# A two-layer transformer on one core: the planned order takes in the load queue, and one number's sigmoid moves to the opening

## The chip, the cores and the metric

The kernel runs on one core of one Trainium2 chip. What counts is the device time of one execution, in microseconds (us); the time of a kernel is the median of its runs. A core has five engines that run their own instruction streams and wait for each other by semaphores: TensorE (PE, matmuls; its loads of the stationary operand are listed as PEld), VectorE (DVE), ScalarE (ACT), GpSimd (POOL) and SyncE (SP). SP does no arithmetic here: it issues the DMAs, that is the loads from and stores to the memory outside the core; POOL issues the indirect ones (gathers and scatter-adds of rows).

## The reference: what is computed

The input `x` has 8 sequences of 1024 rows of 256 numbers (f32). Two layers follow each other, each with four blocks, and each block adds its result to x after a layer norm:

```
x = x + attention_a0(ln(x))      # layer 0: attention in chunks of 64 rows, one head of 256
x = x + experts(ln(x))           # 8 experts, each takes 128 rows of every sequence
x = x + attention_b0(ln(x))      # Fourier chunks of 64: low part attention, high part convolution
x = x + experts(ln(x))           # the same experts again
x = x + attention_a1(ln(x))      # layer 1: linear attention of second order, 16 heads of 32
x = x + ffn(ln(x))               # three 256 x 256 products, bias, tanh
x = x + attention_b1(ln(x))      # window attention, 16 heads of 16, window 128
x = x + ffn(ln(x))
```

Of layer 0, what the change touches:

```
experts:  S = softmax(x Wg^T) over 8 experts; G, I = top 128 rows of each expert
          out[I] += G * (gelu(x[I] W1 + b1) W2 + b2)          # W1 256 x 1024, W2 1024 x 256
attention_b0, in chunks of 64 rows:
          X = rfft(chunk); low = X[:4], high = X[4:]
          A_low = block-causal attention(low) (16 heads of 64), real and imaginary parts alike
          H = pw(gelu(causal depthwise convolution of high, 7 taps dw)) * sigmoid(mean(chunk) gate_w^T)
          y = irfft(alpha * A_low + (1 - alpha) * low, H + high),   alpha = sigmoid(alpha_raw), one number
```

## The kernel before

All matmuls are in f32, and each is a step of some 128 x 128 blocks on PE. Layer 0 is written as a set of chains (Python generators), each of which asks for one piece of work after the other:

- `attention_a` (line 812 on) loads its weights `w1` and `bqk` (names in the trace: `w<-in_wqkv_a_dram`, `bqk<-in_bqk_a_dram`), then for 16 groups of four 128-row tiles it asks for a load of x (`x_a`, L829) and starts a `group`: layer norm on DVE and POOL (`ln4`, L439 statistics, L443 aggregate, L447 power on POOL, L452 apply), transposes on PE (`transposed`, L489; copies out L476 on ACT and L478 on DVE), q and k, v, scores, softmax, p v, and then a `tail`.
- `tail` normalises the result for the next block (tiles `txn_a`, `txn_b`), stores x and the normalised rows (L961, L970), transposes them and makes the routing logits (`put_logits`, L534 to L551).
- `route`, `expert_weights`, `expert_fetch` and `expert_work` are one round of the experts for a half of four sequences. The routing takes the softmax of the logits (`pr`, ACT exp at L581, DVE L582 to L584), transposes it on PE (L592), finds the top 128 on DVE and makes indices. The fetch gathers rows by POOL (L691, tile `xg`) and transposes them on PE (L489 again). The work is 8 `w1` steps (L722) with a gelu on ACT (L732), then `w2` steps (L761), gated on DVE (L771, tile `y`) and scattered by POOL (L778). Weights come through six buffers `we`, loaded by SP (L677). There are four rounds: two halves behind attention a, two behind attention b.
- `attention_b` (line 986 on) starts when all groups of attention a have been asked for and stored. It loads its weights by plain `load`s (helper at line 339, issue at L341) in this order: fourier, qw, kvw, ow, pw, gw, dw. Then it makes alpha:

```
alpha = w["alpha"] = wp.tile([P, 1], F32, tag="alpha", name="alpha")
nc.sync.dma_start(alpha, a["alpha"].partition_broadcast(P))                          # L1005
t = op("alpha", "ACT", 0.22, [], lambda: nc.scalar.activation(alpha, alpha, AF.Exp, scale=-1.0), table="exp")
def sigmoid():
    nc.vector.tensor_scalar(alpha, alpha, 1.0, None, ALU.add)                        # L1016
    nc.vector.reciprocal(alpha, alpha)
events["alpha"] = [op("alpha", "DVE", 0.15, [t], sigmoid)]
```

  The one reader is `dlow` (L1288), which scales the low part. Then, sequence by sequence, it starts chains of `spectrum`, the low attention (q, k, v, with the spread of k into `kbd` at L1228, scores L1309, softmax L1321, `low`), `convolution` (seven taps on DVE, L1369 and L1382), `gates` (sigmoid of the mean, L1418), `pw` and `hs` (L1133), and the inverse transform with its `tail`.

*What sets the order.* The class `Machine` (line 163 on) is a planner that runs while the program is built. It keeps a clock for each engine. Every piece of work has an engine, a cost in us (PE's in passes of 0.109 us), needs (earlier works), slots (numbered buffers) and a name; a load or a store has a `delay` until it has landed. `LAG` adds the time between an engine's end and another's start. In each turn `candidates` picks for each engine the work with the lowest start plus rank, where the rank is a number by name from `RANKS0` (layer 0) or `RANKS` (layer 1), adds 1.295 where ACT has to load another table, and 0.093 or 0.13 where a PE step has another tile shape than the one before. The earliest start of all is taken, and its instructions are issued. So the rank tables and the costs decide the whole order, on every engine.

The order in which the instructions are issued is kept for the engines named in one line (L1436): `with tc.manual_schedule(engines={EN.PE, EN.DVE, EN.Activation, EN.Pool}):`. SP is not among them: its loads and stores are placed by the framework's own scheduler. Loads that aren't asked of the planner (`load`) have no place in its clock; a step that reads such a tile waits for it by a semaphore, without the planner knowing.

Layer 1 (`layer1`, line 1441 on) has a planner of its own with the table `RANKS`, over loops of pairs of chunks. PE works there in three shapes: whole (128 x 128), rows (32 x 128 and the like) and columns (128 x 32). Its steps: transposes of normed rows (L1585), of k (L1806) and of `wt` (L1883), projections (L1765 to q and k, L1786 to v), `head_products` of q, k and u (L1663, the shape rows, four PSUM banks at once, which DVE empties with a mask each, L1671), sums over states and columns (L1689, L1701, L1717, L1727), the state (L1921, L1930), the output product `ho` (L2005), and the window attention's scores (L2144), transposes (L2215) and products (L2253).

Of the kernel before, what the change touches and what calls it, by code (L numbers as in the profile page):

```python
# [10 lines left out]
F32 = mybir.dt.float32  # L11
# [3 lines left out]
AF = mybir.ActivationFunctionType  # L15
ALU = mybir.AluOpType
# [4 lines left out]
P = 128  # L21
B = 8
S = 1024
D = 256
# [6 lines left out]
KS = 7  # L31
# [54 lines left out]
def _constants():  # L86
# [33 lines left out]
    "a add": 0.8, "a columns": -8.0, "a columns copy": -7.2, "a ex columns": 0.85, "a exp": -1.1,  # L120
    "a ln aggr": -2.75, "a ln apply": -0.65, "a ln pow": -0.6, "a ln stats": 0.4, "a max": 1.7,
    "a pt": -1.5, "a pv": -6.35, "a qk": 8.0, "a scores": 2.25, "a sum": -0.4, "a tail columns": -0.3,
    "a tail columns copy": 2.8, "a tail ln aggr": 0.25, "a tail ln apply": -1.55, "a tail ln pow": 3.5,
    "a tail ln stats": 2.0, "a v": 1.35, "a v bias": 1.9, "alpha": 1.1, "b add": -0.4, "b ex columns": 1.3,
    "b exp": -1.4, "b gelu": 0.1, "b k": -8.0, "b k spread": 6.1, "b ln aggr": -3.2, "b ln apply": 0.2,
    "b ln pow": -5.55, "b ln stats": 6.7, "b max": 5.05, "b ot": 6.55, "b pt": 4.45, "b pv": 5.2,
    "b q": -1.0, "b q scale": 2.0, "b scores": -0.4, "b spectrum": -6.25, "b spectrum copy": -2.8,
    "b sum": 2.9, "b tail columns": -4.55, "b tail columns copy": 2.0, "b tail ln aggr": -2.6,
    "b tail ln apply": 8.0, "b tail ln pow": -1.55, "b tail ln stats": 2.75, "b v": -2.15, "b v copy": -4.7,
    "b x add": -1.9, "convolution": 0.8, "cur": -0.85, "cv zero": 3.3, "dlow": -0.3, "gate": -1.6,  # L130
    "gates": -4.0, "gates add": -2.05, "gates exp": -4.1, "gates reciprocal": 6.45, "gates spread": 0.1,
    "gates store": 6.65, "hs": 6.95, "lo": 0.05, "load": -7.15, "logits": 6.15, "logits copy": 1.35,
    "low": 2.9, "lt": -6.6, "lt columns": 4.7, "mt": -7.65, "pr columns": -1.1, "pw": 5.05, "round": 1.95,
    "route exp": -1.15, "route max": 3.2, "route sum": -0.8, "scatter": -0.55, "store x": 1.6,
    "store xn": -0.1, "top": -0.05, "w1": 8.0, "w1 gelu": 5.95, "w2": 1.55, "weights": -0.7,
    "xg columns": 0.05, "xg columns copy": 1.3, "y": 6.1,
}
RANKS = {
    "bout": 4.6, "divide": 3.85, "dk": -0.25, "dq": -2.65, "dq scale": 0.8, "ex columns": 5.2, "exp": -0.4,
    "f_xt aggr": 7.15, "f_xt apply": -0.25, "f_xt columns": -1.35, "f_xt copy": 4.35, "f_xt pow": 2.75,  # L140
    "f_xt stats": -3.9, "ffn0": -4.05, "ffn0 add": 1.55, "ffn0 tanh": -1.4, "ffn1": 6.15, "ffn1 add": -1.6,
    "ffn1 tanh": 3.75, "fold": 8.0, "ho": 0.2, "ho add": 7.95, "in": -7.2, "kt": -3.75, "kt copy": 7.9,
    "kw": -7.6, "kw copy": 0.25, "l_xt aggr": -2.55, "l_xt apply": -0.65, "l_xt columns": 0.3,
    "l_xt copy": 0.8, "l_xt pow": 8.0, "l_xt stats": -3.55, "maximum": -6.3, "o0": 0.35, "ot copy": -0.45,
    "out": -0.3, "pt copy": -0.85, "pt second": 0.15, "pv": 3.9, "pv copy": -0.45, "qt": 5.55,
    "qt copy": 0.4, "reciprocal": 7.9, "scores": 0.15, "sk": -0.7, "sk mask": -0.2, "sp": -6.2,
# [183 lines left out]
def model(ctx: ExitStack, tc: tile.TileContext, a: dict, out: bass.AP):  # L330
# [29 lines left out]
    with tc.tile_pool(name="mk", bufs=1) as mk:  # L360
        mask_rows = load("mask_rows", [P, MASK_ROWS.shape[1]], a["masks"], pool=mk)
        for name, (lo, hi) in MASK_COLS.items():
            masks[name] = cpool.tile([P, hi - lo], BF16, tag=name, name=name)
            nc.vector.tensor_copy(masks[name], mask_rows[:, lo:hi])
# [2009 lines left out]
```

## Time and profile before

| | us |
|---|---|
| median of 3 runs (lowest, highest) | 3726.31 (3726.29, 3729.12) |
| the profiled execution, and its span | 3728.96, 3727.1 |
| PE busy in the span | 3580.6 (96%) |
| DVE, ACT, POOL busy | 2399.8 (64%), 1537.8 (41%), 1265.5 (34%) |
| PE busy from 0 to 30 us | 17.62 |
| PE busy from 30 to 315 (attention a) | 258.27 of 285 |
| PE busy from 315 to 430 (first routings) | 92.30 of 115 |
| PE busy from 430 to 630 (experts) | 200.00 of 200 |
| PE busy from 630 to 1300 (attention b and experts) | 641.03 of 670 |
| PE busy from 1300 to 1675 (last routings, experts) | 355.89 of 375 |
| PE busy from 1675 to 1800 (opening of layer 1) | 117.93 of 125 |
| PE busy from 1800 to 3640 (layer 1) | 1830.37 of 1840 |
| PE busy from 3640 to 3727 (its tail) | 67.15 of 87 |

The profile lists one execution. Its page has busy times, the span in slices and the chain of work that ended last; the trace behind it answers for windows of time, for waits (what an engine stood idle for, and what released it) and for the timeline (start, length, engine, line, what was written from what, and in brackets the idle time before and its releaser). The releaser is inferred from semaphores: where several ended a wait, the one that came last by the records is named. "PEclk" is the clock that TensorE was granted, 1.00 at full speed. An idle engine that isn't the bottleneck costs nothing.

### The profile page before, as it was taken

What the parts mean: (1) busy time and instruction counts of PE and PEld (TensorE: products, weight loads), DVE (VectorE), ACT (ScalarE), POOL (GpSimd) and SP (SyncE); (2) the same over time, 40 slices, a digit from 0 to 9 for tenths busy, and PEclk for the clock granted to TensorE, in tenths of its full rate; (3) what the DMA queues carried; (4) which work ended last, traced back from release to release, by engine and by line L of the source; (5) the groups of instructions that cost most, each with busy time, mean ns of one, the idle gap of its engine ahead of it and who ended that gap; (6) DMA issues with size and microseconds to landing.
All of it is one profiled execution on the core that took longest, in us unless ns stands there. A gap on an engine that the chain in (4) does not pass through costs nothing.

```text
span 3727.1 us, 101090 instructions
## 1 busy us (share of the span) xinstructions
PE 3580.6 (96%) x43080; PEld 2691.6 (72%) x43080; DVE 2399.8 (64%) x5653; ACT 1537.8 (41%) x4724; POOL 1265.5 (34%) x1326
## 2 busy tenths in 40 slices
PE   8898899999999999999999999999999999999997
PEld 5665566676677766667787878787778787878785
DVE  5576615675777672014777777777777777777776
ACT  2232223333143322212554555555555555555545
POOL 1003345242433245531233333333333333333334
PEclk9999999999999999999999999999999999999998
DMA  4213444334524344430000000000000000000000
GB/s 138 79 51 107 135 112 123 87 97 112 124 77 112 95 139 117 120 74 4 2 8 14 9 14 8 14 8 14 8 14 8 14 8 11 11 10 9 6 8 13
DMA packets 164145, 196.94 MB, mean 53 GB/s; under 512 B 11248, under 2 KB 141296, under 8 KB 163696
## 3 DMA queue, kind: packets, MB, share of 16 engines
q1 hardware_dynamic: 139120, 156.92, 13.5%
q0 software_dynamic: 24576, 33.57, 5.2%
q8 instruction: 339, 5.55, 0.6%
q14 instruction: 110, 0.90, 0.1%
HBM read 131.60 MB, written 58.85 MB: 51 GB/s over the span
## 4 chain that ended last, share of the span: by engine, by line
PE 48%; DVE 2%; ACT 1%; issue 0%; POOL 0%; POOLq 0%; DVEq 0%; ACTq 0%
PE acc L1765 5%; PE acc L1663 5%; PE acc L1701 5%; PE acc L2253 3%; PE acc L1616 3%; PE acc L2144 3%; PE acc L1786 3%; PE acc L2005 3%; PE acc L2215 2%; PE acc L1689 2%; PE acc L2274 2%; PE acc L1585 2%; PE acc L1727 2%; PE acc L2060 2%; PE acc L2035 1%; PE acc L1717 1%
## 5 line engine op out<-in xcount | busy, mean ns | idle before, releaser
L722 PE MATMUL acc<-xgt,we 128*128 128x512 f32 x1024 | 460.2, 602 | 0.0
L761 PE MATMUL acc<-we,ht 128*128 128x256 f32 x2048 | 454.6, 382 | 0.0
L2224 POOL TENSOR_TENSOR w_pt<-w_pt,w_above 128x512 f32<-128x512 f32 x256 | 322.7, 1275 | 338.8 <-ACT w_pt L2221 338.5
L2178 ACT ACTIVATE w_ex<-acc,w_nm 128x128 f32<-128x128 f32 x1024 | 362.1, 377 | 182.0 <-DVE w_nm L2170 114.8
L732 ACT ACTIVATE ht<-acc,b 128x512 f32<-128x512 f32 x256 | 175.8, 687 | 618.6 <-PE acc L722 618.1
L761 PEld LDWEIGHTS acc<-we,ht 128*128 128x128 f32 x2048 | 390.0, 192 | 53.8 <-issue 2.8
L722 PEld LDWEIGHTS acc<-xgt,we 128*128 128x128 f32 x1024 | 193.0, 193 | 223.3 <-issue 216.7
L1671 DVE TENSOR_TENSOR sk<-acc,consts 128x512 f32<-128x512 f32 x256 | 164.4, 682 | 157.2 <-PE acc L1663 157.2
L447 POOL TENSOR_TENSOR ln<-ln,nhalf 128x4 f32<-128x4 f32 x64 | 65.2, 1019 | 508.8 <-DVE ln L444 434.5
L1765 PE MATMUL acc<-l_xt,hw 128*128 128x256 f32 x1024 | 236.2, 384 | 0.8 <-ACT l_xt L1593 0.8
L2170 DVE TENSOR_REDUCE w_nm<-acc 128x2 f32<-128x256 f32 x512 | 217.5, 425 | 17.7
L2221 ACT COPY w_pt<-acc 128x512 f32<-128x512 f32 x256 | 141.0, 588 | 194.3 <-PE acc L2215 191.8
L2178 ACT ACTIVATION_READ_ACCUMULATOR w_ex<-acc,w_nm 128x1 f32 x1024 | 220.7, 216 | 0.0
L2195 DVE TENSOR_TENSOR w_ex<-w_ex,w_den 128x512 f32<-128x512 f32 x256 | 213.6, 834 | 8.8
L1765 PEld LDWEIGHTS acc<-l_xt,hw 128*128 128x128 f32 x1024 | 190.9, 191 | 31.4 <-ACT w_pt L2221 6.5
L771 DVE SCALAR_TENSOR_TENSOR y<-acc,gate,gb 128x256 f32<-128x256 f32 x128 | 60.7, 477 | 226.8 <-PE acc L761 178.7
L1671 DVE TENSOR_TENSOR sr<-acc,consts 128x512 f32<-128x512 f32 x256 | 161.2, 682 | 51.5 <-PE acc L1663 51.4
L778 POOL DMA_INDIRECT xa<-y,index x64 | 101.9, 1592 | 237.0 <-DVE y L771 229.3
L778 POOL DMA_INDIRECT xb<-y,index x64 | 101.7, 1589 | 229.9 <-DVE y L771 227.1
L1671 DVE TENSOR_TENSOR sp<-acc,consts 128x512 f32<-128x512 f32 x256 | 161.4, 683 | 14.8 <-PE acc L1663 14.7
L1956 POOL COPY state_bd<-state 32x128 f32<-32x128 f32 x224 | 64.1, 286 | 311.5 <-DVE state L1941 257.5
L1558 POOL TENSOR_TENSOR ln<-ln,nhalf 128x2 f32<-128x2 f32 x128 | 102.4, 800 | 198.7 <-DVE ln L1555 194.3
(260 smaller groups left out, 7902.6 us busy)
## 6 DMA issues: line engine op xcount, KB each, us to landing
we<-in_W_dram SPq DMA_DIRECT2D x128, 512.0 KB, 4.2
x_a<-in_x_dram SPq DMA_DIRECT2D x16, 512.0 KB, 4.4
xa<-x SPq DMA_DIRECT2D x16, 512.0 KB, 5.2
xna<-txn_a SPq DMA_DIRECT2D x16, 512.0 KB, 2.9
x_b<-xa SPq DMA_DIRECT2D x16, 512.0 KB, 4.8
gb<-g SPq DMA_DIRECT2D x32, 256.0 KB, 5.5
xb<-x_b SPq DMA_DIRECT2D x16, 512.0 KB, 2.8
xnb<-txn_b SPq DMA_DIRECT2D x16, 512.0 KB, 3.6
```

Source lines behind the costliest of these rows:

```text
L722: nc.tensor.matmul(ps, w1e[:, k, (f % 4) * P : (f % 4 + 1) * P], xgt[:, k, :], start=k == 0, stop=k == 1,)
L732: nc.scalar.activation(h, ps, AF.Gelu_apprx_tanh, bias=b1[:, col : col + 1])
L761: nc.tensor.matmul(ps[:, :D], ht[f][:, j * P : (j + 1) * P], r["w", e][2 + f // 4][:, f % 4, :], start=f == 0, stop=f == F // P - 1,)
L778: nc.gpsimd.indirect_dma_start(out=x_dram[HB * half + j][:], out_offset=bass.IndirectOffsetOnAxis(ap=index, axis=0), in_=rj["y"], in_offse ...
L1663: nc.tensor.matmul(ps[:, g * P : (g + 1) * P], lhs[rs, g, :], rhs[rs, g, :], start=True, stop=True)
L1671: nc.vector.tensor_tensor(dst, ps.rearrange("p (g t) -> p g t", t=P), bc4(const(mask)), ALU.mult)
L1701: nc.tensor.matmul(ps[32 * g : 32 * g + 32, 0:P], lhs(g, h), rhs[h][:, g, :], start=fresh, stop=i == len(cols) - 1, skip_group_check=True,)
L1765: nc.tensor.matmul(ps[:, gi * 256 : (gi + 1) * 256], hw[:, k, g * 384 + col : g * 384 + col + P], xt[:, k, :], start=k == 0, stop=k == 1,)
L2170: nc.vector.tensor_reduce(nm, sc[:, :, 0, :], AX.X, ALU.max, negate=True)
L2178: nc.scalar.activation(ex[:, 2 * jj + h, :], sc[:, h, 0, :], AF.Exp, bias=nm[:, h : h + 1], accum_out=den[:, 2 * jj + h : 2 * jj + h + 1],)
L2195: nc.vector.tensor_tensor(ex, ex, den.unsqueeze(2).to_broadcast([P, 4, P]), ALU.mult)
L2224: nc.gpsimd.tensor_tensor(pt[:, 1].rearrange("p (j h) t -> p j (h t)", j=2), pt[:, 0].rearrange("p (j h) t -> p j (h t)", j=2), above.rear ...
```

## The change

It has five parts.

1. SP joins the engines whose instructions keep the planner's order in layer 0.
2. Alpha is loaded and made at the very opening of the program, after the masks; `dlow` no longer names it as a need.
3. The weights of attention b become works of the planner on SP, each with a cost and a delay, in the order fourier, qw, kvw, gw, dw, ow, pw; the steps that read them name them as needs.
4. Costs: loads and stores of four tiles 2.6 to 3.0 us, "gate b2" 1.1 to 1.08 and a delay of 0.45, the state step "w" 12.2 to 12.4 passes, "o" 24.8 to 25.2, window "scores" 7.0 to 6.7 with the shape "rows" where "whole" stood; `LAG` gets an entry DVE to DVE of 0.12.
5. Both rank tables are replaced.

No arithmetic is added or taken away; the instructions are the same but for their order, and for table loads on ACT, of which the program holds 55 before and 41 after.

```diff
 RANKS0 = {
-    "a add": 0.8, "a columns": -8.0, "a columns copy": -7.2, "a ex columns": 0.85, "a exp": -1.1,
+    "a add": 0.75, "a columns": 1.6, "a columns copy": 0.9, "a exp": -3.5, "a ln aggr": -0.95,
...
 RANKS = {
-    "bout": 4.6, "divide": 3.85, "dk": -0.25, "dq": -2.65, "dq scale": 0.8, "ex columns": 5.2, "exp": -0.4,
+    "bout": 8.0, "divide": -0.05, "dk": 1.85, "dq": -7.8, "dq scale": 0.05, "ex columns": 2.85, "exp": -1.4,
...
     LAG = {
...
+        ("DVE", "DVE"): 0.12,
...
+    alpha = load("alpha", [P, 1], a["alpha"].partition_broadcast(P))
+    nc.scalar.activation(alpha, alpha, AF.Exp, scale=-1.0)
+    nc.vector.tensor_scalar(alpha, alpha, 1.0, None, ALU.add)
+    nc.vector.reciprocal(alpha, alpha)
...
-                                "weights", "SP", 2.6, [], lambda t=t, src=src: nc.sync.dma_start(t, src), delay=2.5
+                                "weights", "SP", 3.0, [], lambda t=t, src=src: nc.sync.dma_start(t, src), delay=2.5
...
-                        t_gb = op("gate b2", "POOL", 1.1, [("b2", s, half, e)], gated, ("gb2",))
+                        t_gb = op("gate b2", "POOL", 1.08, [("b2", s, half, e)], gated, ("gb2",), delay=0.45)
...
-                    alpha = w["alpha"] = wp.tile([P, 1], F32, tag="alpha", name="alpha")
-                    nc.sync.dma_start(alpha, a["alpha"].partition_broadcast(P))
...
-                    events["alpha"] = [op("alpha", "DVE", 0.15, [t], sigmoid)]
+                    w = {}
+
+                    def weight(name, shape, src, cost):
+                        t = w[name] = wp.tile(shape, F32, tag=name, name=name)
+                        events[name] = [op("weights b", "SP", cost, [], lambda: nc.sync.dma_start(t, src), delay=2.5)]
...
+                    weight("fourier", [P, FOURIER.shape[1]], a["fourier"], 3.6)
+                    weight("qw", [P, 2, 4 * D], rows_of("qw"), 5.2)
...
-                        t = yield step("b spectrum", 8, t_n, ("acc",) if h or k else ("acc", "xf"))
+                        t = yield step("b spectrum", 8, [*t_n, "fourier"], ("acc",) if h or k else ("acc", "xf"))
...
-                t = op("dlow", "DVE", 0.4, [t, "alpha"], scaled, ("dlow",))
+                t = op("dlow", "DVE", 0.4, [t], scaled, ("dlow",))
...
-            with tc.manual_schedule(engines={EN.PE, EN.DVE, EN.Activation, EN.Pool}):
+            with tc.manual_schedule(engines={EN.PE, EN.DVE, EN.Activation, EN.Pool, EN.SP}):
...
-                            "w0" if first else "w",
-                            8.4 if first else 12.2,
+                            8.4 if first else 12.4,
...
-                            t = yield step("scores", 7.0, needs, slots, feeds=2.2)
+                            t = yield step("scores", 6.7, needs, slots, "rows", 2.2)
```

## The prediction

> **What bounds the kernel now.** The page first: TensorE is busy 96% of a 3727.1 us span, and in the chain that ended last every other engine has 2% or less. So a time is lost or won here as TensorE's idle time, or as time between its matmuls. Second, the table of stretches, to see where the idle time lies (two of its rows here, layer 0's worst and the bulk of layer 1); its columns are the stretch, its length, the busy us of PE, PEld, DVE, ACT and POOL, then PE's granted clock, the DMA share and GB/s.
>
> ```profile
> 315.00:430.00 115.00, 92.30 (x461) 61.04 (x462) 62.20 (x162) 28.46 (x45) 46.77 (x44) 0.85 0.51 149
> ...
> 1800.00:3640.00 1840.00, 1830.37 (x32964) 1465.22 (x32959) 1362.67 (x3305) 970.58 (x3468) 626.56 (x702) 1.00 0.03 10
> ```
>
> Of 3727.1 − 3580.6 = 146.5 us idle, 12.4 lies before PE's first matmul (12.38), 9.6 the long stretch of layer 1 and 20 its last 87 us; nearly all the rest lies in layer 0, which ends near 1675. Third, what TensorE waited for in layer 0 (total us, times, longest):
>
> ```profile
> PE acc L592 <- DVE pr L584: 21.6, 3, 15.4
> PE acc L489 <- DVE txn_a L452: 17.3, 7, 2.8
> ...
> PE acc L489 <- DMA xg<-xnb,index: 12.4, 8, 4.1
> ```
>
> One wait of 15.4 us stands out. Fourth, the timeline around it (start, us, engine, line, what; idle before it in brackets):
>
> ```profile
> 386.24 1.31 SPq L1005 DMA_DIRECT2D alpha<-in_alpha_dram  x1
> ...
> 394.55 1.28 ACT L1011 ACT_TABLE_LOAD   x1 [17.15 <-DMA we<-in_W_dram]
> 395.84 0.20 ACT L1011 ACTIVATE alpha<-alpha 128x1 f32<-128x1 f32 x1
> 396.07 0.15 DVE L1016 TENSOR_SCALAR alpha<-alpha 128x1 f32<-128x1 f32 x1 [17.00 <-ACT alpha L1011]
> ...
> 401.21 1.87 PE L592 MATMUL acc<-consts,pr 128*32 128x128 f32 x8 [15.42 <-DVE pr L584]
> 402.87 5.69 PE L722 MATMUL acc<-xgt,we 128*128 128x512 f32 x8
> ```
>
> Read it from the bottom. PE waits for the probabilities `pr` of a routing; they stand on ACT and DVE behind alpha, a sigmoid of one number; alpha's load is the last of eight that SP issues from 378.72 (1 of 0.5 KB, 7.7 us from issue to landing). ACT stood still 17.15 us and DVE 17.00. The releaser named, `we`, isn't what ACT's line reads: L1011 reads alpha, and alpha's landing (386.24 + 7.7 = 393.9) fits its start. After the gap eight matmuls of L722 take 5.69 us, where eight before it took 3.60: a clock loss of 2.1.
>
> **The change part by part.** The sum stands against the profiled execution, 3728.96 us (span 3727.1 and 1.86 around it); it is 2.65 above the median 3726.31 and inside the three runs.
>
> *Alpha at the opening.* Gone from the middle: the 15.4 us wait and the 2.1 of half clock. What is late next: the routing's own chain. Counted from PE's arrival at 385.8 (401.2 − 15.4): a gelu in progress 0.69, a table load 1.28, exp 0.42, sum, reciprocal and product about 1.2, of which some 3.1 lies beside PE's work ahead of the step; 0.5 is left (0 to 4). So −17.0 (−13.5 to −17.5). At the opening alpha costs one DMA issue (about 0.45 on SP, as its neighbours there), 0.20 on ACT and 0.15 + 0.16 on DVE, in the wait for the first x: nothing. If that cover were gone, 0.5.
>
> *SP in the planned order.* Before, two loads of x stand ahead of the first layer's weights; in the built order of the new kernel both weights loads stand ahead of all x.
>
> ```profile
> 3.09 0.98 SPq L829 DMA_DIRECT2D x_a<-in_x_dram  x2
> ...
> 7.97 0.23 DVE L378 CAST ones<-on 128x128 bf16<-128x128 f32 x1
> 8.22 0.37 SPq L341 DMA_DIRECT2D w<-in_wqkv_a_dram  x1
> ...
> 8.82 1.41 DVE L439 BATCH_NORM_STATS2 ln<-x_a 128x6 f32<-128x256 f32 x4 [0.63 <-DMA x_a<-in_x_dram]
> ```
>
> The weights' load waits for the cast that ends at 8.20, so the first x goes out at about 9.1 instead of 3.1. It lands 4.4 later (median of x_a) at 13.5; its statistics began at 8.82. PE's start at 12.38 moves by that: +4.5 (2.8, if the mask lands sooner in a shorter queue; 6.5, if the 768 KB of weights ahead slow it). The weights of attention b go out at the same place, with at least 12 us of PE work between issue and first use; the first x of attention b has 5.3 us of PE work between issue and use (10 before) against 4.8 to land: 0 (0 to +2).
>
> *Layer 0 redrawn.* Every order on every engine comes from new rank tables, so each wait is looked up in the new order.
> - Attention a: seven waits of about 2.5 us (17.3) for `txn_a`, in a period of 20.5 us a group. DVE waits in its order for an x load (4.16 us in one group) with the tail's statistics behind it. In the new order these four statistics come first, so `txn_a` is ready about 2 us sooner, but in every second group its transposes also come sooner, right behind those of x. My chain by hand of two groups gives 40.2 us for 41.1: −0.5 a group, −4 over some eight (−10 to +2).
> - Gathers: the transposes of gathered rows (L489) wait for an indirect load. At the first (3.72), both experts' transposes stood ahead of the first w1; now four w1 steps stand between: −4 (−5 to 0). At two later ones, gaps of 4.07 and 3.84 now have two w1 (1.8 us) in them: −3.6 (−5 to 0).
> - The last routing: its gap near 1340 is 5.95, behind DVE copies for layer 1. PE's steps between the logits' transpose and the probabilities' grow from 3.6 us to some 7.5: −4 (−6 to 0).
> - Attention b: eight gaps, 18 us, partly for the spread of k (kbd), which stood behind 6-tap runs of 3.94 us on DVE. Now two convolution chains alternate and the spread stands ahead: −6 (−14 to +6, as these DVE chains also gate the pw step).
> - Tile shapes on PE: the new order changes shape 205 times where the old did 174, by 17 returns to the full shape. From rows of like steps, leaving the full shape costs 0.093 us (eight matmuls of 256 columns 1.729 to 1.822 until the next) and returning 0.056 to 0.104: +3.
>
> *Costs and lag.* Those constants are the planner's; no instruction has them. Their effect is the order, counted here.
>
> *Layer 1 redrawn.* It has nearly no idle time to win: 9.6 in 1840. Its shape changes go from 1140 to 1200, departures from the full shape from about 13 to 15 in each repeat of two chunks (63.3 us, about 30 repeats). The price of one full-shape step between others, start to start, in the old order:
>
> ```profile
> 2619.60 0.66 PE L1806 MATMUL acc<-consts,kt 128*128 128x128 f32 x4
> 2620.19 1.17 PE L1663 MATMUL acc<-qt,kt 32*128 32x128 f32 x32
> 2621.29 0.66 PE L1585 MATMUL acc<-consts,xn 128*128 128x128 f32 x4
> 2621.78 1.89 PE L2005 MATMUL acc<-ho,ot 128*128 128x256 f32 x8
> ```
>
> Four transposes take 0.59 to the next start when the shape changes (L1806) and 0.49 when it doesn't (L1585). Two more departures and returns a repeat: 2 × (0.12 to 0.21) = 0.24 to 0.42 us, +8.6 to +12.7 over 30 with the odd ones; up to 9 of idle time may close. I take +7 (0 to +14). The Trainium skill, "TensorEngine Tiling (Array Packing)", Key Properties, says that a change of tiling mode, not of the tile alone, drains the engine: a rule against this change. It gives no price; the row above agrees in sign at 0.1 us.
>
> Sum: −17 + 4.5 − 4 − 4 − 3.6 − 4 − 6 + 3 + 7 = −24.1; 3729.0 − 24.1 = 3704.9 on the profiled execution's scale. The median lies up to 2.65 lower, so I say 3704.
>
> The 2.1 us of half clock are seen once in these rows. The Trainium skill, "TensorE: Matmul & The Clock Gate", Part 1, says that an idle window of about 3.4 us halves the clock until about 3.4 us of work has passed, so about 1.7 us; by it, as an estimate, each of the four gaps of 3.7 to 5.95 above would give 1.7 more, and the sum would be some 7 lower.
>
> **The rivals.**
> 1. *The order closes most small waits.* If attention a gives its 10, attention b its 14, the gathers 10 and the last routing 6, with the +4.5, +3 and +7, it is −17 + 14.5 − 40 = −42.5: 3686. For it: each of these waits has a changed order ahead of it. Against: DVE's x_a loads stay just in time, about 4 us of PE work between issue and use, 4.4 to land.
> 2. *Only alpha counts.* The order wins nothing in layer 0 (a wait closed here opens there) and costs 4.5 + 3 + 7: −17 + 14.5 = −2.5: 3726. For it: some 89 us of idle time (146.5 less 12.4, 9.6, 20 and 15.4) stood in an order that keeps to the same dependences.
> 3. *The other side: PE waits for DVE in layer 1.* The new order moves the head products (L1663) close behind the projections of q and k; each takes four of eight PSUM banks, which DVE's masks (0.68 us each) free, and DVE is busy 74% there (1362.67 of 1840). A wait of w a repeat adds 30w; the sum passes +7.5 at w = (24 + 7.5) / 30 = 1.05 us. At 1.35, two masks' time, it is −24 + 40 = +16: 3745. Against: DVE has 16 us of slack in a repeat, and before only 9.6 us of idle show in the whole stretch.
> 4. *The change doesn't do what it says.* Alpha goes, but `pr` is as late, since the redrawn ACT queue has other work ahead of it, or it waits behind the eight loads in another form. Then alpha gives 0 to −4: −24 + 15 = −9, 3720. Against: nothing in the built order ahead of that exp names alpha or those weights.
>
> **How the numbers follow.** Forecast (3690 to 3718) 0.50; rival 1 0.12; rival 4 0.10; rival 2 0.15; rival 3 0.13. Three runs of one kernel spread by 2.8 us, so I hold 0.2%, 7.5 us, for what can be told from no change: faster is below 3718.9, slower above 3733.8. Faster: 0.50 + 0.12 + half of rival 4 and a fifth of rival 2, 0.70; same: the rest of these two, 0.17; slower: 0.13. Eight in ten of the chance lie from 3680 (rival 1 with one more of its bounds) to 3732 (rival 2 with layer 1's +14), which leaves rival 3 out. The likeliest case by itself is 3690 to 3718.
>
> **What would show it.** In the new profile: no alpha line after 15 us; the wait of L592 on `pr` near 390 under 4 us, and eight L722 after it at 3.6 us; PE's first matmul near 16.9; fewer than seven `txn_a` waits of over 2 us; the two 4 us gather gaps near 2; the routing gap near 1340 under 3; PE busy in the long stretch of layer 1 above 99.4%, its length grown by about 7. It is wrong if that stretch grows by tens of us (rival 3), or if a wait of over 10 us stands again near 390 (rival 4).

## The result, and the profile after

The changed kernel takes 3674.02 us (median of 4 runs, 3671.57 to 3675.74) where the kernel before takes 3726.79: a ratio of 0.9855, with a 95% interval from 0.9842 to 0.9867. That is 52.8 us less, and faster by 6 us than the lower end of the predicted range. In two later sessions the same changed kernel took 3680.46 and 3680.48 beside 3728.17 and 3727.99 for the kernel before, so a difference of under some 7 us between sessions says nothing; variants are compared below with a run of the same session where there is one.

The profiled execution took 3672.32 us. The first part of its page, the span and TensorE's busy time:

```profile
span 3670.5 us, 101245 instructions
...
PE 3570.6 (97%) x43080; PEld 2678.6 (73%) x43080; DVE 2379.5 (65%) x5653; ACT 1521.4 (41%) x4710; POOL 1332.2 (36%) x1326
```

Two things moved that the diff does not name: PE is busy 10 us less with the same matmuls, and POOL 67 us more with the same instructions. The table of stretches after the change (stretch, length, busy us of PE, PEld, DVE, ACT, POOL, then PE's granted clock, DMA share, GB/s). Layer 1 starts at 1623.1 now (1675.4 before), so its bulk is 1748 to 3588:

```profile
0.00:30.00 30.00, 12.72 (x37) 6.98 (x38) 14.58 (x60) 5.41 (x8) 4.22 (x10) 1.00 0.80 264
300.00:430.00 130.00, 119.67 (x528) 81.69 (x527) 90.92 (x183) 32.31 (x53) 61.80 (x56) 0.95 0.54 154
...
1748.00:3588.00 1840.00, 1835.24 (x32818) 1467.34 (x32810) 1357.10 (x3307) 973.12 (x3470) 626.17 (x702) 1.00 0.03 10
3588.00:3670.00 82.00, 57.41 (x612) 40.37 (x608) 53.20 (x136) 43.16 (x170) 39.75 (x33) 0.89 0.03 11
```

The first routings have lost half of their idle time and their slow clock (0.95 for 0.85); the bulk of layer 1 has 4.8 us idle for 9.6. What PE waited for in layer 0 (total us, times, longest; a line number is 4 higher than before, 9 lower from attention b's middle on):

```profile
PE acc L493 <- DVE xn_a L456: 17.3, 1, 17.3
PE acc L493 <- DMA xg<-xnb,index: 10.0, 7, 2.2
PE acc L1057 <- DVE xn_b L456: 7.4, 5, 2.2
PE acc L493 <- DMA xg<-xna,index: 6.2, 4, 3.9
...
PE acc L493 <- DVE txn_a L456: 5.7, 11, 1.1
PE acc L596 <- DVE pr L588: 3.2, 1, 3.2
```

Of the same list before the change, three lines that are compared with it:

```profile
PE acc L489 <- DMA xg<-xna,index: 8.3, 7, 3.7
PE acc L1152 <- DVE hs L1133: 7.9, 4, 3.6
PE acc L1309 <- DVE kbd L1228: 7.1, 4, 1.8
```

No wait on `pr` of 15 us, none on `kbd` or `hs`; the opening is longer. The longest wait for a gather of the first half, `xna`, is as long as before (3.9 for 3.7). The timeline of the routing that stood behind alpha:

```profile
369.02 5.32 PE L726 MATMUL acc<-xgt,we 128*128 128x512 f32 x12
...
371.11 0.42 ACT L585 ACTIVATE pr<-pr 128x256 f32<-128x256 f32 x1
...
372.40 0.42 DVE L588 TENSOR_TENSOR pr<-pr,sm 128x256 f32<-128x256 f32 x1
...
374.17 1.04 PE L596 MATMUL acc<-consts,pr 128*32 128x128 f32 x8
...
375.04 5.32 PE L726 MATMUL acc<-xgt,we 128*128 128x512 f32 x12
```

The probabilities are there 1.3 us before PE asks for them, and twelve matmuls behind take 5.32 us where eight took 5.69. And the opening:

```profile
6.63 0.23 DVE L382 CAST ones<-on 128x128 bf16<-128x128 f32 x1
...
6.89 0.38 SPq L341 DMA_DIRECT2D w<-in_wqkv_a_dram  x1
...
7.82 4.69 SPq L833 DMA_DIRECT2D x_a<-in_x_dram  x5
...
13.72 1.41 DVE L443 BATCH_NORM_STATS2 ln<-x_a 128x6 f32<-128x256 f32 x4 [6.59 <-DMA x_a<-in_x_dram]
...
17.28 2.30 PE L493 MATMUL acc<-consts,xn_a 128*128 128x128 f32 x8 [17.28 <-DVE xn_a L456]
```

The first x goes out behind the weights, at 7.82 (3.09 before), and PE starts at 17.28 (12.38).

Put against the prediction's own terms, from the two traces (idle time of PE in front of each kind of matmul, and for the rest the time from each matmul's start to the next start, idle time taken off):

| term | predicted, us | measured, us |
|---|---|---|
| wait for alpha's routing | −14.9 | −15.4 |
| opening | +4.5 | +4.9 |
| attention a: waits on txn_a, ex_a, logits and the like (23.96 to 15.30) | −4 | −8.7 |
| gathers of `xna`, the first among them (8.34 to 6.18) | −4 | −2.2 |
| gathers of `xnb`, the two later gaps among them (12.36 to 10.03) | −3.6 | −2.3 |
| last routing and the two others beside alpha's (6.21 to 3.23) | −4 | −3.0 |
| attention b: hs, kbd, xn_b, ex_b, pt_b (21.85 to 7.87) | −6 | −14.0 |
| small waits (indices, logits) | 0 | −2.1 |
| layer 0, start to start: clock behind alpha −2.1, shapes +3 | +0.9 | −9.6 |
| layer 1: idle −3.5, start to start −0.8 | +7 | −4.3 |
| sum | −24.1 | −56.7 (span: −56.6) |

In the three profiles of the changed kernel the rows of idle time repeat within 1 us, apart from the late copies named at the end of this text; the start-to-start figures do not. Layer 0's start-to-start time is 1565.1 us here and 1560.4 in another profile with the same old layer 0 (the run with layer 1 alone), and 1555.5, 1557.6 and 1559.3 in the three profiles of the changed kernel. So its −9.6 may be anything from −1 to −10. Layer 1 as a whole takes 2051.7 us before, and 2047.5, 2051.6 and 2048.4 in the three profiles of the changed kernel: −4.3 is the largest difference that these give.

### The profile page after: what moved, and what is told of

Its sections match the earlier page's. It is cut to its first block, busy times and chain, and to the rows that moved or that the text cites. A ratio compares the mean times of both kernels' runs of the same rounds, so it can differ in the third digit from the quotient of the medians.

```text
span 3670.5 us, 101245 instructions
## 1 busy us (share of the span) xinstructions
PE 3570.6 (97%) x43080; PEld 2678.6 (73%) x43080; DVE 2379.5 (65%) x5653; ACT 1521.4 (41%) x4710; POOL 1332.2 (36%) x1326
## 4 chain that ended last, share of the span: by engine, by line
PE 88%; DVE 6%; DMA 2%; issue 2%; POOL 1%; ACT 0%; SPq 0%; POOLq 0%; DVEq 0%; ACTq 0%
PE acc L765 11%; PE acc L726 11%; PE acc L1756 6%; PE acc L1654 6%; PE acc L1692 5%; PE acc L2206 3%; PE acc L1777 3%; PE acc L2244 3%; PE acc L1996 3%; PE acc L2135 3%; PE acc L1607 3%; PE acc L1680 2%; PE acc L2265 2%; PE acc L851 2%; PE acc L1718 2%
## 5 line engine op out<-in xcount | busy, mean ns | idle before, releaser
L2215 POOL TENSOR_TENSOR w_pt<-w_pt,w_above 128x512 f32<-128x512 f32 x256 | 332.9, 1316 | 362.3 <-ACT w_pt L2212 362.3
L1756 PE MATMUL acc<-l_xt,hw 128*128 128x256 f32 x1024 | 245.4, 389 | 1.5 <-ACT l_xt L1584 1.5
L2169 ACT ACTIVATION_READ_ACCUMULATOR w_ex<-acc,w_nm 128x1 f32 x1024 | 228.8, 223 | 0.0
L1549 POOL TENSOR_TENSOR ln<-ln,nhalf 128x2 f32<-128x2 f32 x128 | 89.9, 702 | 367.9 <-DVE ln L1546 293.3
L2158 DVE COPY_PREDICATED acc<-consts,acc 128x128 f32<-128x128 int32 x512 | 147.0, 287 | 22.9 <-PE acc L2135 22.5
```

The costliest lines, as they stand in the source:

```text
L1756: nc.tensor.matmul(ps[:, gi * 256 : (gi + 1) * 256], hw[:, k, g * 384 + col : g * 384 + col + P], xt[:, k, :], start=k == 0, stop=k == 1,)
L2169: nc.scalar.activation(ex[:, 2 * jj + h, :], sc[:, h, 0, :], AF.Exp, bias=nm[:, h : h + 1], accum_out=den[:, 2 * jj + h : 2 * jj + h + 1],)
L2215: nc.gpsimd.tensor_tensor(pt[:, 1].rearrange("p (j h) t -> p j (h t)", j=2), pt[:, 0].rearrange("p (j h) t -> p j (h t)", j=2), above.rear ...
```

## Experiments: alpha

**Alpha alone.** The kernel before, with this part of the change and no other:

```diff
+    alpha = load("alpha", [P, 1], a["alpha"].partition_broadcast(P))
+    nc.scalar.activation(alpha, alpha, AF.Exp, scale=-1.0)
+    nc.vector.tensor_scalar(alpha, alpha, 1.0, None, ALU.add)
+    nc.vector.reciprocal(alpha, alpha)
...
-                    alpha = w["alpha"] = wp.tile([P, 1], F32, tag="alpha", name="alpha")
-                    nc.sync.dma_start(alpha, a["alpha"].partition_broadcast(P))
```

> The kernel before with alpha loaded and made at the opening; rank tables, costs, SP and weights as before. Theory 1 (the 15.4 us wait of L592 and the half clock behind it, 2.1 to 2.6, are alpha's alone and nothing takes their place): 16 to 18 us less than before, 3709 to 3711; PE's first matmul stays near 12.4. Rival (the probabilities would be late anyway, on ACT or DVE or behind the loads of attention b's weights): a wait of over 5 us stays there and the gain is under 12 us, 3715 or more.

Measured: 3709.46 beside 3726.23, a ratio of 0.9958 (0.9944 to 0.9972), 16.8 us. In the timeline of this run PE's idle time there is 0.89 (15.42 before):

```profile
385.03 0.42 DVE L588 TENSOR_TENSOR pr<-pr,sm 128x256 f32<-128x256 f32 x1
385.60 1.03 PE L596 MATMUL acc<-consts,pr 128*32 128x128 f32 x8 [0.89 <-DVE pr L588]
386.47 5.32 PE L726 MATMUL acc<-xgt,we 128*128 128x512 f32 x12
```

The prediction's 0.5 us of remaining wait and its −17 hold (the interval is 10 to 21 us). Layer 0's idle time falls by 13.6 us here (110.3 to 96.7). Its start-to-start time reads 1560.9, but the run with layer 1 alone, of the same session and with the 15.4 us gap still in it, has 1560.4; so the 2.1 us of slow running behind the gap are all that is shown of it.

**Alpha put back.** The changed kernel with alpha's load and operations at the start of attention b again; PE's order is the same, instruction for instruction.

> The changed kernel with alpha's load and its three operations put back to the start of attention b, PE's order the same instruction for instruction. Theory 1: the wait for the second routing's probabilities is back at 8 to 16 us with up to 2.6 of slow clock behind it, the time is 10 to 18 us above the changed kernel's 3674. Rival (the new order hides alpha's load): within 4 us of 3674.

Measured: 3683.07. The wait for `pr` is back with 3.74 us, less than 8 to 16, since alpha's load now goes out ahead of attention b's weights, which are the planner's works by then, and not behind seven of them. Against the changed kernel's 3674.02 this is 9 us, against its later sessions 2.6: an estimate of alpha's worth inside the new order lies between these. The changed kernel was not run beside this variant, so the wait of 3.74 us is the better figure. Most of the 15.4 us lay in the place at the end of the load queue.

## Experiments: the opening and SP's order

**x first.** The changed kernel, with the first two loads of x sent ahead of attention a's weights:

```diff
-                    w1 = load(
-                        "w1", [P, 2, 3 * D], a["wqkv_a"].rearrange("(k p) e -> p k e", p=P), pool=wpool
-                    )
-                    bqk = load("bqk", [P, 4], a["bqk_a"], pool=wpool)
+                    def fetch(x, g):
+                        nc.sync.dma_start(x, x_rows[g])
+                        if g == 1:
+                            nc.sync.dma_start(w1, a["wqkv_a"].rearrange("(k p) e -> p k e", p=P))
+                            nc.sync.dma_start(bqk, a["bqk_a"])
```

> The changed kernel with the first two loads of x ahead of the loads of attention a's weights, as they stood before; PE, ACT and POOL in the same order. Theory 1 (the opening's 4.9 us are the order of these loads): PE's first matmul back at 12.4 from 17.3, the time 4.9 us less, 3669. Rival (the weights then come late and the loss moves to the first projection): PE's first matmul near 12.4, a wait of 3 to 5 us at the first projection, and the time within 2 us of 3674.

Measured: PE's first matmul at 12.28, no wait at the first projection, the experts' first step at 321.2 (326.4): the opening is as predicted. But the time was 3678.29, 4.3 more than the 3674.02, and there was no run of the changed kernel in that session. So it was run again:

> The changed kernel itself, beside the others on the same chip, as the yardstick for differences of a few us from it. If the 4 us that the run with x first lost are that kernel's, this one stays within 2 us of 3674; if they lie in the chip or the hour, it is at 3677 to 3679.

Measured: 3680.46. The same kernel thus differs by 6.4 us between two sessions, and the 4.3 us of the variant are within that. What x first is worth in time by itself, no run of one session shows.

**More loads behind x.** As x first, with the loads of `rows`, the gate's weight and the first bias behind it too.

> The changed kernel with the first two loads of x ahead of attention a's weights and of the loads of rows, gate and first bias too; PE, ACT and POOL in the same order. Theory 1: x goes out 1.3 us sooner than in the run with x first, PE's first matmul at 10.9 to 11.5 instead of 17.3 to 18.2, the first step of the experts 6 us sooner than 327, and the time 5 to 7 us less than the changed kernel beside it. Rival (mask and weights bind then): PE starts sooner but waits for the weights, at most 4 us gained.

Measured: first matmul at 11.04, the experts' first step at 321.0, the time 3674.62 in a session without the changed kernel; against 3680.5 of the sessions around it, 5.9 less, which is within what sessions differ by.

**SP free again.** The changed kernel with SP left out of the engines that keep the planner's order; 48 lines of SP's order differ, and none of PE, ACT and POOL. Its yardstick, the changed kernel in the same session, comes first:

> The changed kernel itself, the yardstick for the three others on this chip: 3672 to 3681, where its runs have been so far.

> The changed kernel with SP left out of the engines that keep the planner's order, as before; PE, ACT and POOL in the same order, 48 lines of SP's differ. Theory 5 (SP's part of the change costs the opening and gives nothing): PE's first matmul back near 12.4, no load of x, of weights or of attention b late, the time 0 to 5 us less than the yardstick. Rival (the planned order of loads and stores is what lets the new order run): waits for x or weights come back, 5 us or more above the yardstick.

Measured: 3673.44 beside 3680.48, 7.0 us less. The first rows of PE in the two timelines, this variant and then the yardstick:

```profile
12.75 1.66 PE L493 MATMUL acc<-consts,xn_a 128*128 128x128 f32 x5 [12.75 <-DVE xn_a L456]
```

```profile
17.51 1.87 PE L493 MATMUL acc<-consts,xn_a 128*128 128x128 f32 x6 [17.51 <-DVE xn_a L456]
```

So the part of the change that the title names first costs the opening, 4.8 us, and no run shows it to give anything back. The runs of the two kernels overlap a little (3672.1 to 3677.9, and 3676.5 to 3684.1), so I count 5 to 7 us. The whole change is faster in spite of it.

## Experiments: attention b

The trace after the change shows something that the prediction had named but not priced. Before, the seven taps of one convolution chain follow each other on DVE, each waiting for the last. After, two chains alternate. The groups of taps, before and after (count, busy us, mean ns, idle):

```profile
L1382 DVE SCALAR_TENSOR_TENSOR cv<-xf,dw,cv 128x448 f32<-128x448 f32 (+2 forms) x192 | 126.6, 660 | 6.6
```

```profile
L1373 DVE SCALAR_TENSOR_TENSOR cv<-xf,dw,cv 128x448 f32<-128x448 f32 (+2 forms) x192 | 106.8, 628 | 0.0
```

From start to start, first taps included and idle time taken off, that is 0.627 us each before and 0.544 after, 18.6 us over 224; with the idle time, some 0.04 us between two taps of one chain, it is 0.656 before. What lets the planner see it is the entry of 0.12 us from DVE to DVE in its table of lags: two works in line on one engine no longer look as if they could follow at once, so the next tap of another chain is picked first. That is read from the code; no run takes the entry out. Two runs take the taps by themselves. The places of the taps in DVE's order are kept, and only which tap is issued in which place is changed:

```diff
-                        t = op("convolution", "DVE", 0.365, [*needs, "dw"], first)
+                        taps.append(first)
+                        t = op("convolution", "DVE", 0.365, [*needs, "dw"], issue)   # issue: taps.pop(0)()
```

**Serial taps in the changed kernel.**

> The changed kernel with the convolution's taps on DVE put back one chain after the other in the same places of DVE's order; every other instruction of every engine stands where it stood. Theory 2 (what empties attention b's waits is that two chains of taps alternate, 0.544 us a tap for 0.627 in the traces): DVE busy grows by 15 to 19 us, waits at the scores or the inverse transform return, and the time is 6 to 14 us longer, 3680 to 3688. Rival (the place of the spread and of hs in DVE's order does it, the taps lie beside PE's work): at most 3 us longer.

Measured: 3703.44 beside 3680.46, 23 us longer, more than the 6 to 14 expected. What PE waits for from 560 us to layer 0's end in this run, and then in the yardstick:

```profile
PE acc L1143 <- DVE hs L1124: 15.4, 6, 2.7
PE acc L493 <- DMA xg<-xnb,index: 10.5, 8, 2.2
PE acc L1057 <- DVE xn_b L456: 9.4, 5, 3.0
```

```profile
PE acc L493 <- DMA xg<-xnb,index: 9.9, 7, 2.2
PE acc L1057 <- DVE xn_b L456: 7.8, 5, 2.8
```

The wait for `hs` is there with 15.4 us. Layer 0's idle time grows by 18.3 us (69.0 to 87.3) and its start-to-start time by 10.7.

**Alternating taps in the kernel before.**

> The kernel before with the same taps alternating between two chains in the same places of DVE's order, nothing else moved. Theory 2: DVE busy falls by 15 to 19 us, the waits of kbd (7.1 us in all) and hs (7.9) go for the most part, 8 to 14 us less than before, 3713 to 3719. Rival: waits stay, within 3 us of 3727.

Measured: 3724.05 beside 3728.17, a ratio of 0.9991 (0.9982 to 1.0), so a gain of 0 to 7 us where 8 to 14 were expected. The waits of `kbd` are gone and those of `hs` fall from 7.9 to 1.6, as theory 2 has it. But two new ones of 6.9 us come. The timeline at the first:

```profile
617.25 1.89 POOL L691 DMA_INDIRECT xg<-xna,index  x1 [0.30 <-issue]
...
619.45 9.76 POOL L691 DMA_INDIRECT xg<-xna,index  x1 [0.30 <-issue]
621.03 0.81 DVE L1374 TENSOR_SCALAR cv<-xf,dw 128x464 f32<-128x464 f32 x2
621.76 6.62 DVE L1388 SCALAR_TENSOR_TENSOR cv<-xf,dw,cv 128x448 f32<-128x448 f32 x12
...
631.29 0.21 POOL L1099 COPY lo<-xf 128x48 f32<-128x48 f32 x1
...
631.56 2.72 PE L1199 MATMUL acc<-lo,qw 128*128 128x128 f32 x11 [6.88 <-POOL lo L1099]
```

A gather on POOL takes 9.76 us, as long as DVE runs taps without a pause; in the kernel before, the same gather beside serial taps takes 0.95:

```profile
617.83 0.95 POOL L691 DMA_INDIRECT xg<-xna,index  x1 [0.30 <-issue]
```

Behind it on POOL stand the copies of the low part `lo`, and PE waits for these. In the changed kernel the same happens eight times (5.65 us twice, 9.56 six times; the sum over all gathers and scatters is 396 us for 333, which is 63 of POOL's 67 us of added busy time), but there PE's list has no wait for POOL, so nothing that PE needs soon stands behind the gather. So neither the taps nor the order alone gives attention b's 14 us of idle time: the new order needs quick taps (23 us without), and quick taps in the old order gain 4.

## Experiments: attention a

**A sixth buffer for x.** The kernel before, with one number changed (22 lines of PE's order follow):

```diff
-                    "x_a": 5, "xn_a": 2,
+                    "x_a": 6, "xn_a": 2,
```

> The kernel before with six buffers for x in attention a instead of five, so that each load goes out a group earlier; 22 lines of PE's order differ. Theory 3 (DVE waits in its order for a load of x that is just in time, the tail's statistics wait behind it, and txn_a is late for that): the seven txn_a waits (17.3 us) fall below 4 in all, and with what runs slowly behind each (1.1 us of eight transposes at 1.73 for 1.04 and the like) 14 to 22 us less than before, 3705 to 3713. Rival (DVE has too much to do between, the load only covers it): the waits keep more than half, under 8 us gained, 3719 or more.

Measured: 3723.61 beside 3728.17, a ratio of 0.9986 (0.9978 to 0.9995). The waits on `txn_a` keep 15.4 of 17.3 us. The edit did not do what it was for: the planner starts a group's statistics as early as its load allows, so with a buffer more DVE waits for the load of a later group in the same place (3.94 us, for 4.16). The theory is not tested by it. The experts' first step comes at 319.0, 8 us sooner, of which about 4 are idle time.

**The tail's statistics first.** The kernel before with two ranks of the new table:

```diff
-    "a ln stats": 0.4, "a tail ln stats": 2.0,
+    "a ln stats": 1.3, "a tail ln stats": 0.9,
```

> The kernel before with two ranks of the changed kernel's table, so that DVE takes the tail's four statistics ahead of those of x in attention a; 148 of 13438 lines of PE's order move with it, all in attention a. Theory 3 (the tail's statistics queue behind DVE's wait for a load of x, and txn_a is late for that): the txn_a waits (17.3 us in seven) fall below 6 in all, attention a ends 8 to 16 us sooner, 3711 to 3719. Rival (the late txn_a only hands its wait to the next step in line, as the buffer and tap runs did): the sum of idle time in attention a falls by less than 5 us, 3722 or more.

Measured: 3734.24 beside 3729.73, a ratio of 1.0012 (1.0004 to 1.0021): slower. What PE waits for in the first 600 us:

```profile
PE acc L534 <- DVE txnt_a L478: 15.6, 5, 7.2
PE acc L634 <- DVE idxf L630: 13.7, 1, 13.7
...
PE acc L489 <- DVE txn_a L452: 7.4, 11, 1.1
```

The theory holds where it was meant: `txn_a` is ready sooner (7.4 us for 17.3), and between its first matmul and 300 us PE stands idle 8.1 us for 22.3 before. The 14 us are lost again after it. The five waits for `txnt_a` (15.6) all lie between 316 and 338 us, where the first routing's search for the top 128 (L614 to L624 on DVE) now stands between the copies of the last tails. The 13.7 us in front of the indices are alpha's wait in another place: DVE stands still 12.75 us at L1016 for alpha, up to 353.0, and the indices' cast follows at 353.27; the wait of 15.4 us for `pr` is not in this list. No run joins these two ranks with alpha at the opening.

**Attention a's ranks put back in the changed kernel** (the names that begin with a; 172 of 13438 lines of PE's order differ):

> The changed kernel with the ranks of attention a alone (the names that begin with a) put back; 172 of 13438 lines of PE's order differ, all in attention a. Theory 6 (the new order of attention a is itself worth what its idle time fell by, 8.6 us, and the slow running behind): the first step of the experts comes 8 to 14 us later than the yardstick's 327, the time is 8 to 14 us longer. Rival (the lag and the corrected costs, which stay, did it): within 3 us.

Measured: 3695.48 beside 3680.48, 15.0 us longer; layer 0's idle time is 14.2 us more. The mark that was set, a later first step of the experts, failed (316.4, sooner, as the order of the two works changes too); the end of the first round of experts comes 16.5 us later. So attention a's order as a whole, with the first routing that runs into it, is worth some 15 us inside the changed kernel. Which of its ranks bring this, no run takes apart.

**A sixth buffer in the changed kernel,** and then together with x first:

> The changed kernel with six buffers for x in attention a instead of five. Before the change this gave 8 us up to the first step of the experts (319.0 for 327.1). Theory 3b (DVE's wait for x is still in the new order): the first step of the experts comes 4 to 8 us sooner than 327. Rival (the new order has taken that gain): within 2 us of 327, the time as the changed kernel's.

Measured: first step at 321.1, 6 us sooner than 327; the time is 3679.47, nothing to tell from the yardsticks of other sessions.

> The changed kernel with both edits that brought the experts' first step forward by 6 us each: x loaded first, and six buffers for x. Theory 7: they add, the first step is at 315 to 316, and 4 to 8 us remain at the end, 3668 to 3674 where the yardstick is at 3676 to 3680. Rival (what is won early is lost again by the end of layer 0, as each alone lost most of it): within 3 us of the yardstick.

Measured: first step at 316.8 (9.5 us sooner than the yardstick's 326.2), 3674.07 beside 3680.48, 6.4 us less. It is no faster than SP free alone: what is won early is lost in part by the end of layer 0.

## Experiments: layer 1

**Layer 1 alone.** The kernel before with the new `RANKS`, three costs and the lag there; its layer 0 is the old one in every instruction's place.

> The kernel before with the changed kernel's layer 1 alone (its rank table, its three costs, the lag between two operations of DVE there); layer 0 as before. Theory 1, from the two traces (layer 1 takes 2051.7 us before and 2047.4 after): 4.3 us less than before, 3722. Rival, the prediction's own price (each more return to the full shape paid in full): 7 us more, 3734. A second rival, that layer 1 gains only behind the new layer 0: no difference, 3727.

Measured: 3722.07 beside 3726.23, a ratio of 0.9989 (0.9980 to 0.9998), so 4.2 us less (0.7 to 7.5): near the traces' 4.3, and the other sign than the prediction's +7. Layer 1's idle time shows it in every profile: 29.0 to 30.7 us in the five with the old order, 23.9 to 26.2 in the twelve with the new one. Its start-to-start time does not tell the two apart (2020.2 to 2023.5 us, and 2021.3 to 2025.7). The prediction's count of shape changes was the mistake. Taken from all changes of shape in the two traces of layer 1 (mean of the time from the last matmul of a group to the next start, over the usual distance in that group; F is 128 x 128, R 32 x 128, C 128 x 32):

```
change       before            after             sum after - before
F to R      223 x  94 ns      254 x  93 ns       +2.7 us
F to C      113 x  95 ns      140 x  93 ns       +2.4
R to F      255 x 220 ns      280 x 216 ns       +4.4
C to F      161 x 199 ns      195 x 188 ns       +4.8
C to R       96 x 193 ns       65 x 192 ns       -6.1
R to C       33 x 205 ns        7 x 237 ns       -5.1
F to F      589 x  44 ns      560 x  33 ns       -7.2
```

The prediction counted 59 departures and 59 returns, priced a little low at 8.6 to 12.7 us together (14.3 here). It left out that 57 of them stand where a direct change stood, and that such a change costs as much as a return: −11.2. What stays of the shapes is +3 (2.5 to 3.6 between any two profiles of the two orders). Steps that change no shape give −7.2, most of it at the ffn's bias matmuls, for a reason that no run here isolates; but layer 1's start-to-start time as a whole falls by only 0.8 in these two profiles, and in most other pairs it does not fall. The Trainium skill, "TensorEngine Tiling (Array Packing)", Key Properties, says that a change of mode drains the engine. The runs are in line with it, and put the numbers beside it: some 0.09 us to leave the full shape, some 0.2 to return, and some 0.2 between two others.

**Fewer changes of shape.** The changed kernel, with the planner's price of a change tripled in layer 1:

> The changed kernel with the planner's price of a change of shape tripled in layer 1: 61 fewer departures from and returns to the full shape, 72 more direct changes between two other shapes. Theory 4, by the prices of the two traces (departure 0.094 us, return 0.19 to 0.21, direct change 0.19 to 0.21): layer 1's matmuls take 3.6 us less from start to start, and idle time grows or falls beside it by what the trace will show. Rival, the prediction's price (a departure and a return together 0.15 to 0.21, direct changes not counted): 9 to 13 us less.

Measured: 3956.13, 280 us longer. The shapes cannot be read from it, for PE waits everywhere. What it waits for in layer 1, and one stretch of it (columns as above; the changed kernel has 399.30 of 400 busy in the same stretch, at a clock of 1.00):

```profile
PE acc L1577 <- DVE xn L1555: 52.4, 55, 3.5
PE acc L2245 <- POOL w_pt L2216: 34.0, 41, 2.0
PE acc L2207 <- DVE w_ex L2187: 23.7, 12, 3.2
```

```profile
2000.00:2400.00 400.00, 364.42 (x5729) 283.82 (x5718) 264.98 (x637) 194.36 (x692) 127.61 (x133) 0.95 0.04 10
```

This is the rival of the other side, of another place: waits of 1 us for DVE and POOL in each repeat. One constant of the planner brings them on, and they go with 150 us of idle time and 120 us of slower running beside it. The whole order of layer 1 moved with that constant, so this run shows how much hangs on the order, not what a shape change costs.

## Why the prediction was right or wrong

The sign was right, the time was not: 3704 with a range from 3680 to 3732, measured 3674. By the table the sum is 32.6 us short. The largest misses are layer 1 (11.3), layer 0's start-to-start time (10.5, of which up to 8.5 may be the execution), attention b (8.0) and attention a (4.7).

- **Alpha**, −17: right. Alone it gives 16.8 us, PE's remaining wait is 0.89 us for the 0.5 said, and nothing takes its place.
- **SP in the planned order**, +4.5: right in mechanism and size (+4.9), and the run with SP free shows it from the other side, 7.0 us.
- **Gathers and the last routing**, −11.6: right in sign, −7.5 in size. At the first gather the step failed: the gap of 3.72 us is 3.87 now, for the four w1 steps stand behind the first expert's transposes, and only the second expert's three waits (2.3 us) are gone. At the two later gaps the reading was right: the two w1 steps take them from 4.07 and 3.84 to 2.14 and 2.24, but behind the first of them a new wait of 2.13 stands. The last routing's gap went from 5.95 to 3.23.
- **Attention a**, −4: the sign holds, the size was −8.7 of idle time and about 15 us with all that hangs on it. The step that failed is the chain by hand of two groups, which gave 0.5 us a group: in the run with the tail's statistics first the same move takes some 14 us off PE's idle time up to 300 us, and in the changed kernel this time is 10.8 us less (11.5 for 22.3). The chain by hand also ended before the last groups, where the first routing meets the tails on DVE.
- **Attention b**, −6 (−14 to +6): the largest term that was mis-sized, −14.0 of idle time. The sum said "two convolution chains alternate" and gave this no price, though the trace had the taps at 0.66 us in line. It was 18.6 us of DVE's busy time, and with serial taps the new order loses 23 us.
- **Layer 0's tile shapes**, +3, and 2.1 us of slow clock: the term for all that isn't idle time had the wrong sign, −1 to −10 for +0.9. The shapes themselves cost +4.6, reckoned as in layer 1 (28.3 to 32.9), for most returns took 0.17 to 0.25 us where 0.056 to 0.104 was read. What the sum left out is slow running behind the small gaps. In the 7 us behind each gap of over 1 us matmuls take 41.0 us longer in all than the median of their line before, and 23.7 after (27 gaps, then 14); other pairs of profiles give 12 to 19 for this difference of 17. The sentence that gave each of the four larger gaps 1.7 us was nearer than the sum.
- **Layer 1**, +7 (0 to +14): wrong, −4.2 in its own run. The step that failed is "two more departures and returns a repeat", which counted what the new order adds (14.3 us) and not the direct changes that it takes out (−11.2). What stays, +3, is less than the idle time that closes, some 3 to 7 us.

Rival 1 (the order closes most small waits, 3686) came nearest, and was still 12 us short: its own layer 1 and shapes were those of the forecast. Rival 3 did not come about, but one constant away it does. Rivals 2 and 4 fell by the run with alpha alone and by the waits above. The parts, each from its own run (alpha 17, layer 1 4, attention a 15, taps 23, SP's order −7), add up to 52, near the measured 47 to 53. That is luck as much as proof, as the worth of one part depends on the others: alpha is worth 17 us in the old order and 3 to 9 in the new, the taps 4 in the old and 23 in the new.

## What to carry to other kernels

When a planner's order is redrawn, don't price the waits of the old order one by one: what one edit wins (14 us up to 300 us, by two ranks) can be lost at the next place where two chains meet, and two halves (quick taps, and an order that needs them) may be worth little apart and 20 us together. Count changes of tile shape by kind, from the shape before to the shape after. And look at each queue by itself: here a part of the change that costs 5 to 7 us is hidden in a whole that gains 50.

## What the runs showed of the hardware

- **POOL's gathers stand still beside unbroken DVE work.** A gather of 0.95 us took 9.56 us (13.0 at most, in the run with alternating taps in the old order) while DVE ran two alternating chains of taps, each with two inputs from SBUF; beside serial taps, which leave DVE idle for some 0.04 us between two, no gather took over 1.52. The Trainium skill, "SBUF — State Buffer", Who interferes with whom, says that the two engines share a pair of ports under an exclusive lock that is held for an instruction. The runs agree that one blocks the other; that POOL doesn't get in between 14 or more DVE instructions is more than it says, and no run here isolates why one to three gathers just before took 1.1 to 1.9 us beside the same taps.
- **Idle time of PE goes with slower running behind it.** With 18.3 us of idle time more (serial taps, same session) came 10.7 us of longer running, where executions of one kernel differ by 4; with 150 more (tripled price), 120. Part of it is the granted clock, 0.95 to 0.98 in most of layer 1 in the last. The Trainium skill, "TensorE: Matmul & The Clock Gate", Part 1, puts the fall of the clock at an idle window of about 3.4 us. In the changed kernel a single gap of 2.25 us (up to 578.6) is followed by 3.4 us at a clock of 0.51 and 1.9 us of slow running, and one of 3.23 (up to 1284.1) by a clock of 1.00 and none: the length of the gap alone doesn't decide. Nor is all of it the clock: in the kernel before, eight transposes behind a gap of 2.40 us (at 107.4) take 1.73 us for 1.04, at a clock of 1.00.
- **A late copy that comes and goes.** In some executions, with the same instructions in the same order, DVE's copy of a routing's logits starts 1.1 to 2.0 us late, in the same two places; in the two earlier profiles of the changed kernel it did not, in the third it did. In four of the profiles with the new order it starts, at the first of the two places, within 0.1 us of the end of a gather on POOL. What decides it stays open.
